# Normalized offset features turned back to channels, GELU with scale and bias there, and the offset product on TensorE

## The chip, the cores and the metric

The kernel runs on one core of a Trainium2 chip, in one launch. The metric is the time of one execution in microseconds (us) of device time; the figure for a kernel is the median of several executions. Engines are named as in the profile: PE is TensorE (matrix products; PEld are its weight loads), DVE is VectorE, ACT is ScalarE, POOL is GpSimd, SP is SyncE, which here only issues DMAs.

## The reference, cut to what matters

Four images of 32 x 32 pixels with 384 channels pass through four layers, each with a group normalization `_gn` before it and a residual sum. Layer 0 is a deformable attention; the part that the change touches makes its offsets:

```python
q = jnp.einsum('bhwc,cd->bhwd', x, w_q) + b_q
o = lax.conv_general_dilated(q, w_off0, (1, 1), 'SAME', ..., feature_group_count=G) + b_off0
mu = o.mean(-1, keepdims=True)
var = ((o - mu) ** 2).mean(-1, keepdims=True)
o = (o - mu) * lax.rsqrt(var + 0.001) * ln_g + ln_b
o = jax.nn.gelu(o, approximate=False)
o = o.reshape(Bq, Hq, Wq, G, GC)...                 # G = 6 groups of GC = 64 channels
offset = jnp.einsum('bhwc,ct->bhwt', o, w_offp)     # w_offp: 64 x 2, the same for each group
offset = jnp.tanh(offset) * jnp.array([Hq / 2.0, Wq / 2.0], x.dtype)
pos = offset + ref
...
xs = _bilinear_sample(xg, pos)                      # keys and values are made from xs
...
bias = _bilinear_sample(rpe_img, disp)              # disp comes from pos too
```

The rest of layer 0 is an attention of six heads over 1024 keys with that bias. Layer 1 is an attention with a convolution branch and a similarity of groups, layer 2 a box filter, layer 3 a dynamic 3 x 3 convolution. Each layer ends in a residual sum.

## The kernel before

Everything is float32. Channels lie on partitions in KC = 3 tiles of 128 (an image is `[128, 3, 1024]`), or pixels lie on partitions in NJ = 8 tiles of 128 (`[128, 8, 384]`).

Two lanes make the instruction stream. `Front` is layer 0 of an image, `Trunk` layers 1 to 3. Image 0's front runs first and alone. Then a loop takes steps of the trunk of image b and adds steps of the front of image b+1 in proportion to planned costs, the numbers behind each `yield`, so that the front of image 1, 2 or 3 shares the engines with the trunk of the image before it. Within this program a scheduler chooses at build time the order in each engine's queue, except where `keep_in_program_order` (`pin`) holds it. That order is fixed in the built program: in the trace, an instruction that waits holds up those behind it on its engine.

The steps of a front, in `inputs0`, with the lines that the prediction names:

- `normed` loads the image's pixels, turns them to channels (copies by ACT, L570), does the group normalization (bn_stats L313; sums over groups on PE, L343, 14 records a time, with 128x128 weights and one column; root on ACT, L366; scaling on DVE, L374), turns the result to pixels (ACT, L594) and writes it to the table `pairs` in DRAM, from which the samples are gathered. For image 0 it also fills the table's borders (ACT's queue, L237) and makes the table of the position bias: DVE works on it in L185 to L192, ACT's queue writes `half` (L193) and then `strips` (L198, six DMAs).
- The queries: a dense product on PE (L393), copied by ACT into `qpad` (L623, three times).
- The offset convolution, three channel tiles of 72 matmuls each (L642), copied by ACT with its bias (L650).
- 24 transposes to pixels (PE, L661), and copies by ACT into `oall` (L665).
- The layer normalization over channels, all on DVE except the root (ACT, L683): per pixel tile one subtraction of the mean and product with ln_g (L692), and one product with 1/std and sum with ln_b (L695). ln_g and ln_b are rows copied to all partitions, since channels lie along the free axis here.
- GELU on ACT per pixel tile (L699).
- `positions`: for each of the two coordinates one product on DVE of the whole tile with w_offp (L478), and a reduction over each group's 64 channels (L479); Tanh on ACT (L480); the positions (L484) and some forty small DVE operations up to the index of the samples `sidx` (L526) and that of the bias `widx`.
- 48 gathers by POOL (L712), eight blocks of six, weighted on DVE (L725) and turned back to channels by PE (L739).

Image 0 does the normalization, GELU and `positions` in two parts of four pixel tiles; images 1 to 3 in one part of eight. The products (L478) write to a work tile `tmp` that has a buffer of the tag `a12`; there are two of these buffers, and large tiles of the front share them in turn. PSUM has two large buffers of `[128, 1024]` (`big`) and four of `[128, 512]` (`bank`), for both lanes.

While the fronts of images 1, 2 and 3 do these steps, the trunk is at the start of layer 1 (`inputs1`): gate (L393, copies L1142), convolution taps on DVE (L1154, L1156), queries and keys by PE (L1168) with copies by ACT or DVE (L1178), norms (L1208 on PE; maximum and reciprocal on DVE, L1220 and L1221), and the first scores (L1322 on PE, maximum on DVE L1330, exponential on ACT L1331).

The functions that the diff touches, and what calls them:

Of the kernel before, what the change touches and what calls it, by code (L numbers as in the profile page):

```python
# [20 lines left out]
AF = mybir.ActivationFunctionType  # L21
ALU = mybir.AluOpType
# [4 lines left out]
P = 128  # L27
# [45 lines left out]
class Net:  # L73
# [33 lines left out]
    def consts(self):  # L107
        nc, a = self.nc, self.a
        self.ident = self.ct([P, P], "ident")
        make_identity(nc, self.ident)  # L110
        self.ones = self.ct([P, P], "ones")
        nc.gpsimd.memset(self.ones, 1.0)
        self.eps = self.ct([P, 2], "eps")
        for i, v in enumerate((1e-5, 1e-3)):
            nc.gpsimd.memset(self.eps[:, i : i + 1], v)

        self.cols = self.ct([P, KC, NCOL], "cols")
        nc.sync.dma_start(self.cols, a["cols"].rearrange("(k p) v -> p k v", p=P))

        self.boff = self.ct([P, KC, 2], "boff")  # L120
        src = a["cols"].rearrange("(k g c) v -> g c k v", g=2, c=GC)
        for g in range(2):
            for h in range(2):
                nc.scalar.dma_start(
                    self.boff[GC * h : GC * (h + 1), :, g], src[g, :, :, C_BOFF]
                )
        self.rows = self.ct([P, NROW], "rows")
        nc.sync.dma_start(self.rows, a["rows"].partition_broadcast(P))
        self.blk = self.ct([P, P], "blk")
        nc.scalar.dma_start(self.blk, a["blk"])  # L130

        self.hsum = self.ct([P, 32], "hsum")
        nc.gpsimd.memset(self.hsum, 0.0)
        nc.vector.tensor_copy(self.hsum[:, 0:4], self.blk[:, 0::32])
        self.hall = self.ct([KC * 32, P], "hall")
        nc.gpsimd.memset(self.hall, 0.0)
        for k in range(KC):
            nc.sync.dma_start(self.hall[32 * k : 32 * k + 4, :], a["blk"][0::32, :])
        self.sel = self.ct([81, 9, 25], "sel")
        nc.scalar.dma_start(self.sel, a["sel"])  # L140
        self.xmask = self.ct([P, 25], "xmask")
        nc.scalar.dma_start(self.xmask, a["xmask"])
        self.wnorm = self.ct([P, HW], "wnorm")
        nc.scalar.dma_start(self.wnorm, a["wnorm"].partition_broadcast(P))
        nc.vector.tensor_scalar(self.wnorm, self.wnorm, 0.2, None, ALU.mult)
        self.ref = self.ct([P, 2, NJ], "ref")
        nc.scalar.dma_start(self.ref, a["ref"])
        self.gofs = self.ct([P, 2, G], "gofs")
        nc.scalar.dma_start(self.gofs, a["gofs"].partition_broadcast(P))
        for g in range(G):  # L150
            nc.gpsimd.memset(self.gofs[:, 1, g : g + 1], float(g * NSTRIP * STRIP))

        self.wa = self.ct([P, KC, 81], "Wa")
        nc.sync.dma_start(self.wa, a["Wa"].rearrange("(k p) d -> p k d", p=P))


        self.gam = self.ct([P, 2], "gam")
        nc.scalar.activation(
            self.gam[:, 0:1], self.rows[:, R_SCAL + 2 : R_SCAL + 3], AF.Sigmoid
        )  # L160
        nc.vector.tensor_scalar(
            self.gam[:, 1:2], self.gam[:, 0:1], -1.0, 1.0, ALU.mult, ALU.add
        )

        self.half = self.ct([P, 2], "half")
        nc.vector.tensor_scalar(
            self.half, self.rows[:, R_SCAL : R_SCAL + 2], 0.5, None, ALU.mult
        )
# [247 lines left out]
class Front(Lane):  # L416
# [48 lines left out]
                nc.sync.dma_start(self.x1[b % 2][rows, :], x)  # L465
                yield 6

    def positions(self, oall, js, tmp, w4, sidx):


        nc, v = self.nc, self.nc.vector
        NC = len(js) * G
        cols = slice(js.start * G, js.stop * G)
        og = oall[:, js.start : js.stop, :].rearrange("p j (g c) -> p (j g) c", g=G)
        th = self.wt([P, 2, NC], "ix_th")
        for t in range(2):
            wrow = self.rows[:, R_WOFFP + t * GC : R_WOFFP + (t + 1) * GC]
            v.tensor_tensor(tmp, og, bc(wrow, 1, NC), ALU.mult)  # L478
            v.tensor_reduce(th[:, t, :], tmp, AX.X, ALU.add)  # L479
        nc.scalar.activation(th, th, AF.Tanh)  # L480
        s = lambda tag, dt=F32: self.wt([P, 2, NC], tag, dt=dt)
        pos = s("ix_pos")
        for t in range(2):
            v.scalar_tensor_tensor(  # L484
                pos[:, t].rearrange("p (j g) -> p j g", g=G),
                th[:, t].rearrange("p (j g) -> p j g", g=G),
                HW / 2.0,
                bc(self.ref[:, t, js.start : js.stop], 2, G),
                ALU.mult,
                ALU.add,  # L490
            )
        qi, gt = s("ix_qi", I32), s("ix_gt")

        def floor(out, q, top):

            v.tensor_copy(qi, q)
            v.tensor_copy(out, qi)
            v.tensor_tensor(gt, out, q, ALU.is_gt)
            v.tensor_tensor(out, out, gt, ALU.subtract)
            v.tensor_scalar(out, out, float(top), 0.0, ALU.min, ALU.max)  # L500


        q, qc, fl, al = s("ix_q"), s("ix_qc"), s("ix_fl"), s("ix_al")
        v.tensor_scalar(q, pos, 0.5, None, ALU.add)
        v.tensor_scalar(qc, q, 0.0, float(HW + 1), ALU.max, ALU.min)
        floor(fl, qc, HW)
        v.tensor_tensor(al, q, fl, ALU.subtract)
        v.tensor_scalar(al, al, 0.0, 1.0, ALU.max, ALU.min)
        one = self.wt([P, 2, NC], "ix_one")
        v.tensor_scalar(one, al, -1.0, 1.0, ALU.mult, ALU.add)  # L510
        edge = self.wt([P, 2, NC], "ix_edge")
        v.tensor_scalar(edge[:, 0, :], fl[:, 0, :], 1.0, None, ALU.is_ge)
        v.tensor_scalar(edge[:, 1, :], fl[:, 0, :], float(HW - 1), None, ALU.is_le)
        wx = self.wt([P, 2, NC], "ix_wx")
        v.tensor_tensor(wx[:, 0, :], one[:, 0, :], edge[:, 0, :], ALU.mult)
        v.tensor_tensor(wx[:, 1, :], al[:, 0, :], edge[:, 1, :], ALU.mult)
        for lr in range(2):
            v.tensor_tensor(w4[:, cols, lr, 0], wx[:, lr, :], one[:, 1, :], ALU.mult)
            v.tensor_tensor(w4[:, cols, lr, 1], wx[:, lr, :], al[:, 1, :], ALU.mult)
        fi = self.wt([P, len(js), G], "ix_fi")  # L520
        fi2 = fi.rearrange("p j g -> p (j g)")

        def index(out, hi, lo, mul, which):
            v.scalar_tensor_tensor(fi2, hi, float(mul), lo, ALU.mult, ALU.add)
            v.tensor_tensor(fi, fi, bc(self.gofs[:, which, :], 1, len(js)), ALU.add)
            v.tensor_copy(out, fi2)  # L526

        index(sidx[:, cols], fl[:, 1, :], fl[:, 0, :], HW, 0)

        u = s("ix_u")
        v.tensor_scalar(u, pos, -1.0, 2.0 * NWIN - 17.0, ALU.mult, ALU.add)
        v.tensor_scalar(u, u, 0.0, 2.0 * NWIN, ALU.max, ALU.min)
        floor(fl, u, 2 * NWIN - 1)
        f = self.f[:, :, :, cols]
        v.tensor_tensor(f[:, 0], u, fl, ALU.subtract)
        v.tensor_scalar(f[:, 1], f[:, 0], -1.0, 1.0, ALU.mult, ALU.add)
        v.tensor_scalar(q, fl, 0.25, None, ALU.mult)
        floor(qc, q, NSTRIP - 1)  # L540
        v.scalar_tensor_tensor(
            fl[:, 0, :], qc[:, 0, :], float(STRIP - 4), fl[:, 0, :], ALU.mult, ALU.add
        )
        index(self.widx[:, 0, cols], fl[:, 1, :], fl[:, 0, :], WROW, 1)

        v.tensor_scalar(fi2, fi2, float(HW // 2 * WROW), None, ALU.add)
        v.tensor_copy(self.widx[:, 1, cols], fi2)
# [60 lines left out]
    def inputs0(self, b):  # L608
# [61 lines left out]

        parts = 2 if b == 0 else 1
        size = NJ // parts
        tmp = self.wt([P, NJ * G, GC], "a12", 2)[:, 0 : size * G]
        w4 = self.wt([P, NJ * G, 2, 2], "w4")
        sidx = self.wt([P, NJ * G], "sidx", 1, I32)
        for part in range(parts):
# [11 lines left out]
            )  # L688
            v.reciprocal(rstd, rstd)
            for i, j in enumerate(js):  # L690
                o = oall[:, j, :]
                v.scalar_tensor_tensor(  # L692
                    o, o, mv[:, j, 0:1], self.rows[:, R_LNG : R_LNG + C], ALU.subtract, ALU.mult
                )
                v.scalar_tensor_tensor(  # L695
                    o, o, rstd[:, i : i + 1], self.rows[:, R_LNB : R_LNB + C], ALU.mult, ALU.add
                )
            for j in js:
                nc.scalar.activation(oall[:, j, :], oall[:, j, :], AF.Gelu)  # L699
            yield 25 / parts  # L700
            self.positions(oall, js, tmp, w4, sidx)
            yield 20 / parts


# [1162 lines left out]
```

## Time and profile before

| | us |
|---|---|
| median of 4 runs | 4708.06 |
| lowest and highest of them | 4704.38, 4716.64 |
| the profiled execution's own time | 4703.28 |
| its span in the profile | 4701.5 |
| PE busy | 4157.6 (88%) |
| DVE busy | 3209.5 (68%) |
| ACT busy | 2295.4 (49%) |
| POOL busy | 944.2 (20%) |

The profiled execution took 1.8 us more than its span, the time that lies outside it. The mean granted clock of PE was 0.927 of the full one. In the rows of the profile a line number such as L479 is a line of the kernel; `out<-in` are the program's tiles, and `xN` says how many instructions the row sums. A timeline's row begins with start and duration in us, and ends, in square brackets, with the time that the engine stood idle before it and what ended that.

### The profile page before, as it was taken

To read this page: it belongs to the slowest core of one execution; us is meant where nothing else is said; L and a number is where in the kernel's file an instruction comes from. 1 tells how busy PE (TensorE), PEld (TensorE's weight loads), DVE (VectorE), ACT (ScalarE), POOL (GpSimd) and SP (SyncE) were. 2 spreads that over 40 slices of the span, in tenths; PEclk is the share of its full clock that TensorE was granted. 3 is DMA by queue.
4 is the path that set the end of the run, shared out by engine and by line. 5 is a ranking of instruction groups with operands and counts; after the bars stand their busy time and mean duration, and the time that the engine had idled before them with its cause. 6 is when DMAs were issued, how large, how long until landed. Compare 5 with 4: busy or idle time off the path is not lost. (4 is left out here: it accounts for less than half of the span.)

```text
span 4701.5 us, 46786 instructions
## 1 busy us (share of the span) xinstructions
PE 4157.6 (88%) x15704; PEld 1781.7 (38%) x15704; DVE 3209.5 (68%) x6013; ACT 2295.4 (49%) x3631; POOL 944.2 (20%) x946
## 2 busy tenths in 40 slices
PE   5477788999999988899999989799999998999998
PEld 2222233333333353333333444343333335343444
DVE  3499755777878727577878753768787784565654
ACT  2166433566665323456666432346565651455532
POOL 1533204211212103311212110422121211000000
PEclk8688988999999988999999989899999998999998
DMA  6435234321212143321212124432121213311011
GB/s 125 131 112 151 69 98 130 90 62 55 70 43 64 63 138 126 109 64 49 82 51 65 49 81 125 147 93 58 29 79 50 75 37 111 110 26 32 19 40 41
DMA packets 231729, 369.98 MB, mean 79 GB/s; under 512 B 117507, under 2 KB 164704, under 8 KB 231488
## 3 DMA queue, kind: packets, MB, share of 16 engines
q1 hardware_dynamic: 170472, 200.51, 14.5%
q0 software_dynamic: 39936, 145.53, 10.4%
q10 hardware_dynamic: 21080, 20.96, 1.8%
q8 instruction: 124, 2.03, 0.2%
q14 instruction: 117, 0.96, 0.1%
HBM read 287.41 MB, written 79.78 MB: 78 GB/s over the span
## 5 line engine op out<-in xcount | busy, mean ns | idle before, releaser
L1479 PE MATMUL bank<-whole,sg 128*128 128x512 f32 (+3 forms) x2304 | 858.4, 507 | 6.3 <-POOL sg L1432 4.4
L1488 DVE SCALAR_TENSOR_TENSOR e<-bank,gam,e 128x512 f32<-128x512 f32 x768 | 561.8, 748 | 439.3 <-ACT gf L1487 157.7
L1331 ACT ACTIVATE big<-big,nmax 128x1024 f32<-128x1024 f32 x384 | 418.7, 1090 | 393.9 <-DVE nmax L1330 346.0
L1457 ACT ACTIVATE e<-big 128x1024 f32<-128x1024 f32 x384 | 379.8, 1019 | 413.4 <-PE big L1449 407.6
L1479 PEld LDWEIGHTS bank<-whole,sg 128*128 128x128 f32 x2304 | 405.3, 198 | 371.1 <-issue 283.1
L1330 DVE TENSOR_REDUCE nmax<-big 128x1 f32<-128x1024 f32 x384 | 454.4, 1218 | 57.6 <-PE big L1322 38.6
L797 POOL DMA_INDIRECT win<-strips,widx x288 | 308.4, 1071 | 684.0 <-DVE z L810 410.9
L1432 POOL TENSOR_SCALAR sg<-whole,gam 128x512 f32<-128x512 f32 x192 | 149.5, 781 | 1451.1 <-PE bank L1479 1014.7
L1449 PE MATMUL big<-qa,ka 64*128 64x512 f32 x1536 | 423.5, 623 | 9.6 <-ACT big L1331 9.3
L1322 PE MATMUL big<-k,q 32*128 32x512 f32 x1536 | 326.1, 680 | 70.5 <-ACT e L1457 40.5
L818 PE MATMUL bank<-qpad,kz 128*128 128x512 f32 x576 | 282.9, 620 | 12.5 <-DVE e L1488 12.5
L712 POOL DMA_INDIRECT gat<-pairs,sidx x192 | 205.4, 1070 | 418.2 <-DVE sidx L526 238.0
L853 PE MATMUL bank<-lg,va 128*64 128x512 f32 x576 | 266.5, 607 | 15.0 <-ACT lg L851 14.9
L853 PE MATMUL bank<-lg,ones 128*64 128x512 f32 x576 | 265.8, 607 | 0.0
L815 DVE SCALAR_TENSOR_TENSOR lg<-z,bias_f,lg 128x512 f32<-128x512 f32 x288 | 220.0, 772 | 39.0 <-ACT lg L814 36.8
L809 ACT ACTIVATE z<-win,bias_f 128x528 f32<-128x528 f32 x288 | 208.2, 738 | 66.4 <-DVE lg L815 30.7
L1449 PEld LDWEIGHTS big<-qa,ka 64*128 64x128 f32 x1536 | 137.9, 186 | 265.9 <-issue 156.2
L810 DVE SCALAR_TENSOR_TENSOR z<-win,bias_f,z 128x528 f32<-128x528 f32 x288 | 214.1, 760 | 26.6 <-ACT z L809 19.4
L850 DVE TENSOR_TENSOR lg<-lg,tb 128x512 f32<-128x512 f32 x288 | 187.1, 695 | 42.4 <-ACT tb L843 42.4
L1421 PE MATMUL bank<-e,vs 128*32 128x512 f32 x1536 | 206.7, 604 | 0.9 <-DVE vs L1415 0.9
L819 DVE TENSOR_TENSOR lg<-bank,lg 128x512 f32<-128x512 f32 x288 | 191.8, 683 | 22.1 <-PE bank L818 21.0
L814 ACT ACTIVATE lg<-z,bias_f 128x512 f32<-128x512 f32 x288 | 200.3, 718 | 12.3 <-PE bank L853 5.6
(302 smaller groups left out, 6634.3 us busy)
## 6 DMA issues: line engine op xcount, KB each, us to landing
pairs<-xn SPq DMA_DIRECT2D x64, 192.0 KB
q<-qd SPq DMA_DIRECT2D x48, 256.0 KB
w<-in_gmat SPq DMA_DIRECT2D x16, 576.0 KB
w<-in_w_off SPq DMA_DIRECT2D x12, 576.0 KB
w<-in_Wqkv SPq DMA_DIRECT2D x12, 576.0 KB
a<-in_x SPq DMA_DIRECT2D x16, 384.0 KB
x<-a ACTq DMA_DIRECT2D x4, 1536.0 KB
win<-strips,widx POOLq DMA_INDIRECT x384
```

Of the source, the lines that this page charges most:

```text
L797: nc.gpsimd.indirect_dma_start(out=win, out_offset=None, in_=self.strips[:, :], in_offset=bass.IndirectOffsetOnAxis(ap=self.widx[:, q, c : ...
L810: v.scalar_tensor_tensor(z, wv[:, 1 : HH + 1, 0 : HW + 1], sc(0, 1), z, ALU.mult, ALU.add)
L815: v.scalar_tensor_tensor(lg, z[:, :, 1 : HW + 1], sc(0, 0), lg, ALU.mult, ALU.add)
L818: nc.tensor.matmul(ps, kz[:, j * P : (j + 1) * P], both, start=True, stop=True)
L853: nc.tensor.matmul(po[out, :], w, lf, start=j == 0, stop=j == NJ - 1)
L1322: nc.tensor.matmul(ps[r][:, h * 512 : (h + 1) * 512], self.q4[rows, i * P : (i + 1) * P], self.k4[rows, 0:512], start=True, stop=True,)
L1330: v.tensor_reduce(nmax[:, r, i : i + 1], ps[r], AX.X, ALU.max, negate=True)
L1331: nc.scalar.activation(ps[r], ps[r], AF.Exp, bias=nmax[:, r, i : i + 1], accum_out=den[:, r, i : i + 1],)
L1449: nc.tensor.matmul(ps[:, r, :], ka[rows, j * P : (j + 1) * P], qa[rows, cols], start=True, stop=True,)
L1457: nc.scalar.activation(e, ps, AF.Exp)
L1479: nc.tensor.matmul(ps[:, (mid - i0) * P :], sg[:, r, m, :], sim[:, h, r, m, (mid - i0) * P :], start=m == 0, stop=m == 1,)
L1488: v.scalar_tensor_tensor(e[:, r, :], ps, self.gam[:, 1:2], e[:, r, :], ALU.add, ALU.mult, accum_out=tot[:, r, h : h + 1],)
```

## The change

After the change the layer normalization in pixels does only its subtraction and product, `(o - mean) * rstd`, as one DVE instruction per pixel tile. 24 transposes on PE, in groups that fill a `big` each, turn the result to channels. There ln_g and ln_b are one number per partition, so that ACT's GELU applies them as scale and bias while it reads PSUM; it writes a tile `ge` that takes the place of `tmp` among the `a12` buffers. The offsets are matmuls: for each pixel tile and channel tile, 128 pixels of `ge` are the weights and a constant `offp` of `[128, 4]` is the moving operand. It holds w_offp for the upper and the lower 64 channels in columns of their own, so that the four results are two coordinates for two groups. The 24 matmuls (12 for each part of image 0) fill one `bank`, and Tanh reads it. `tmp` and DVE's products and reductions are gone. The constants `ln` and `offp` are loaded at the start, by six DMAs on ACT's queue, after a memset by POOL.

```diff
@@ consts
         nc.sync.dma_start(self.rows, a["rows"].partition_broadcast(P))
+        self.ln = self.ct([P, 2, KC], "ln")
+        for i, at in enumerate((R_LNG, R_LNB)):
+            nc.scalar.dma_start(
+                self.ln[:, i, :], a["rows"][at : at + C].rearrange("(k p) -> p k", p=P)
+            )
+        self.offp = self.ct([P, 4], "offp")
+        nc.gpsimd.memset(self.offp, 0.0)
+        for h in range(2):
+            for t in range(2):
+                at = R_WOFFP + t * GC
+                nc.scalar.dma_start(
+                    self.offp[GC * h : GC * (h + 1), 2 * h + t : 2 * h + t + 1],
+                    a["rows"][at : at + GC].rearrange("(c o) -> c o", o=1),
+                )
@@ positions
-    def positions(self, oall, js, tmp, w4, sidx):
+    def positions(self, ge, js, w4, sidx):
...
-        og = oall[:, js.start : js.stop, :].rearrange("p j (g c) -> p (j g) c", g=G)
+        ps = self.bank()
+        for i in range(len(js)):
+            for k in range(KC):
+                at = (i * KC + k) * 4
+                nc.tensor.matmul(
+                    ps[:, at : at + 4],
+                    ge[:, k, i * P : (i + 1) * P],
+                    self.offp,
+                    start=True,
+                    stop=True,
+                )
         th = self.wt([P, 2, NC], "ix_th")
-        for t in range(2):
-            wrow = self.rows[:, R_WOFFP + t * GC : R_WOFFP + (t + 1) * GC]
-            v.tensor_tensor(tmp, og, bc(wrow, 1, NC), ALU.mult)
-            v.tensor_reduce(th[:, t, :], tmp, AX.X, ALU.add)
-        nc.scalar.activation(th, th, AF.Tanh)
+        nc.scalar.activation(
+            th, ps[:, 0 : 2 * NC].rearrange("p (n t) -> p t n", t=2), AF.Tanh
+        )
@@ inputs0
-        tmp = self.wt([P, NJ * G, GC], "a12", 2)[:, 0 : size * G]
+        gelus = self.wt([P, KC, N], "a12", 2)
...
             for i, j in enumerate(js):
-                o = oall[:, j, :]
-                v.scalar_tensor_tensor(
-                    o, o, mv[:, j, 0:1], self.rows[:, R_LNG : R_LNG + C], ALU.subtract, ALU.mult
-                )
-                v.scalar_tensor_tensor(
-                    o, o, rstd[:, i : i + 1], self.rows[:, R_LNB : R_LNB + C], ALU.mult, ALU.add
-                )
-            for j in js:
-                nc.scalar.activation(oall[:, j, :], oall[:, j, :], AF.Gelu)
+                v.tensor_scalar(
+                    oall[:, j, :], oall[:, j, :],
+                    mv[:, j, 0:1], rstd[:, i : i + 1],
+                    ALU.subtract, ALU.mult,
+                )
+            ge = gelus[:, :, js.start * P : js.stop * P]
+            for k in range(KC):
+                ps = self.big()[:, 0 : size * P]
+                for i, j in enumerate(js):
+                    nc.tensor.transpose(
+                        ps[:, i * P : (i + 1) * P], oall[:, j, k * P : (k + 1) * P], self.ident
+                    )
+                nc.scalar.activation(
+                    ge[:, k, :],
+                    ps,
+                    AF.Gelu,
+                    bias=self.ln[:, 1, k : k + 1],
+                    scale=self.ln[:, 0, k : k + 1],
+                )
             yield 25 / parts
-            self.positions(oall, js, tmp, w4, sidx)
+            self.positions(ge, js, w4, sidx)
```

More of the change, by code (lines that the diff above doesn't have):

```diff
@@ L690, in inputs0 @@
             for i, j in enumerate(js):
-                o = oall[:, j, :]
-                v.scalar_tensor_tensor(
-                    o, o, mv[:, j, 0:1], self.rows[:, R_LNG : R_LNG + C], ALU.subtract, ALU.mult
-                )
-                v.scalar_tensor_tensor(
-                    o, o, rstd[:, i : i + 1], self.rows[:, R_LNB : R_LNB + C], ALU.mult, ALU.add
-                )
-            for j in js:
-                nc.scalar.activation(oall[:, j, :], oall[:, j, :], AF.Gelu)
+                v.tensor_scalar(
+                    oall[:, j, :],
+                    oall[:, j, :],
+                    mv[:, j, 0:1],
+                    rstd[:, i : i + 1],
+                    ALU.subtract,
+                    ALU.mult,
+                )
+            ge = gelus[:, :, js.start * P : js.stop * P]
[11 more added lines that the diff above has]
+                    scale=self.ln[:, 0, k : k + 1],
+                )
             yield 25 / parts
-            self.positions(oall, js, tmp, w4, sidx)
+            self.positions(ge, js, w4, sidx)
             yield 20 / parts
```

## The prediction

> **What bounds the kernel now.** I read the engines' busy shares first, then a table of windows round the code that the change touches, then the timelines of those windows. PE is busy 88% of the 4701.5 us span, so over the whole program only time in which PE stands idle, or works for nothing, can be won. But the change touches four stages only, and each has its own limit. The table of windows shows them (columns: window, length, busy us and instruction count of PE, weight loads, DVE, ACT and POOL, then granted clock, DMA share, GB/s):
>
> ```profile
> 0.00:80.00 80.00, 56.77 (x328) 29.57 (x328) 12.14 (x29) 15.70 (x27) 6.56 (x21) 0.89 0.88 170
> 80.00:111.00 31.00, 3.94 (x28) 2.58 (x24) 28.11 (x69) 13.06 (x24) 0.23 (x1) 0.65 0.07 20
> ...
> 660.00:680.00 20.00, 20.00 (x51) 7.54 (x50) 20.00 (x34) 10.86 (x17) 0.00 (x0) 1.00 0.53 149
> 680.00:700.00 20.00, 13.75 (x39) 4.95 (x37) 20.00 (x24) 7.13 (x10) 0.00 (x0) 0.92 0.25 82
> ```
>
> Image 0's front runs alone: from 80 to 111 us DVE is busy 28.11 of 31, PE only 3.94, and the gathers wait for it. Image 1's front shares its time with the trunk: from 660 to 680 PE and DVE are both full, then DVE stays full while PE has gaps. Images 2 and 3 repeat this at about 1800 and 2930 us.
>
> Image 0's chain, from the timeline: last convolution pass, both tanh, the index of part 0, first gather.
>
> ```profile
> 55.28 25.12 PE L642 MATMUL big<-qpad,w 64*64 64x512 f32 x216 [0.52 <-issue]
> ...
> 100.61 0.24 ACT L480 ACTIVATE ix_th<-ix_th 128x48 f32<-128x48 f32 x1 [1.14 <-DVE ix_th L479]
> ...
> 110.31 0.17 DVE L526 CAST sidx<-ix_fi 128x24 int32<-128x24 f32 x1
> ...
> 110.77 1.16 POOL L712 DMA_INDIRECT gat<-pairs,sidx  x1 [91.78 <-DVE ix_fl L497]
> ...
> 112.32 0.24 ACT L480 ACTIVATE ix_th<-ix_th 128x48 f32<-128x48 f32 x1 [8.46 <-DVE ix_th L479]
> ```
>
> The index of part 0 comes 9.7 us after its tanh, because DVE does part 1's work in between. From 110.77 to about 180 us 48 gathers follow one another at some 1.25 us. After them the heads keep DVE busy for 271.35 of the 280 us from 260 to 540. So an earlier first gather moves all that follows, one for one.
>
> The joint stage of image 1, DVE's timeline:
>
> ```profile
> 682.88 3.35 DVE L479 TENSOR_REDUCE ix_th<-a 128x48 f32<-128x3072 f32 x1
> ...
> 687.26 3.34 DVE L1221 RECIPROCAL inv<-inv 96x512 f32<-96x512 f32 x1
> 690.52 0.26 DVE L484 SCALAR_TENSOR_TENSOR ix_pos<-ix_th,ref 128x48 f32<-128x48 f32 x2
> 690.70 1.22 DVE L1330 TENSOR_REDUCE nmax<-big 128x1 f32<-128x1024 f32 x1
> ...
> 693.02 4.95 DVE L1221 RECIPROCAL inv<-inv 96x768 f32<-96x768 f32 x1
> ...
> 701.82 0.19 DVE L526 CAST sidx<-ix_fi 128x48 int32<-128x48 f32 x1
> ```
>
> The tanh runs at 686.25, but its reader L484 stands behind a reciprocal of the trunk until 690.52. So up to 4.27 us of a later tanh are free; what comes later still holds L484, and with it L1330, the second L1221 and the index, all queued behind it on DVE.
>
> **DVE's part of the change.** Per image 8 normalizations of 0.593 us (L692) and 8 of 0.609 us (L695) go: 9.6 us. Eight scalings of 128x384 come instead; L374's 0.81 us for 128x1024 gives an estimate of 0.31 us each, 2.5 us. Two products of 3.35 us (L478) and two reductions of 3.34 us (L479) go too, 13.4 us. DVE is relieved of 9.6 + 13.4 - 2.5 = 20.5 us per image.
>
> **PE's part.** 24 transposes come, like L661's, which issue six in 0.82 us: 0.137 us each, 3.3 us. And 24 matmuls with 128x128 weights and 4 columns in 4-byte numbers. No such shape runs now; the nearest is L343 with one column, 14 records, of which a matmul makes two:
>
> ```profile
> 1556.78 1.72 PE L343 MATMUL bank<-gn_d,w 128*128 128x1 f32 x14
> ...
> 26.58 3.12 PE L343 MATMUL bank<-gn_d,w 128*128 128x1 f32 x14 [0.93 <-DVE gn_d L362]
> ```
>
> That is 0.123 us a record at its fastest and 0.223 us in a cold stretch. 48 records: 5.9 or 10.7 us. PE gains 9.2 us warm, 14.0 cold. In the joint stage I take warm (clock 1.00 from 660 to 680, 0.92 after), in image 0 cold (0.65 from 80 to 111).
>
> [...]
>
> **ACT's part.** Eight GELU of 0.51 us from SBUF (4.1 us) become three of 128x1024 from PSUM; L1331's 1.09 us gives 3.3 us. In image 0 they are six of 128x512, like L650's 0.687 us: 4.1 us. Tanh reads PSUM, 0.28 us as now. So ACT is even. Each GELU now waits for a PSUM buffer that PE must fill, and on ACT the next copies queue behind it; the joint stage has ACT at about half, so I give this nothing, up to 1 us if it is seen.
>
> **Constants.** Six loads of 4-byte elements go on ACT's queue, plus one small memset on POOL. They cost issue time on ACT in the first 15 us, where ACT waits for x anyway (3.11 us before 14.90); uncovered it would be some 0.3 us each (L193's issue), 2 us.
>
> **What moves in image 0's opening.** The rebuilt instruction orders, set side by side, are alike on every engine outside the four stages and the opening. In the opening the work on the rpe table (DVE's L185 to L192, ACT's issue of half) goes behind the group normalization. Now ACT holds its last five copies of x behind it: they wait 2.83 us for DVE's L185 and end at 20.2. Ahead of it they would end at about 18, after x's last landing. Then the six strip loads, which block ACT's queue for 12.64 us now (39.59 to 53.25), stand after the second L623 instead of the first. So the convolution can start at about 48 instead of 55.28, but its second third waits for the third L623, blocked until about 59. I get an end of the convolution near 75.6 instead of 80.33: 4.7 us won. Bounds: nothing, if the third L623 comes late by as much as the first came early, and 7 us, the whole advance of the start.
>
> **Image 0 between convolution and gathers.** From the first transpose back (80.33), the tanh of part 0 comes now at +20.3, that of part 1 at +32.0, the index of part 0 at +30.0. After the change DVE's chain is short: square root at +6.5, the GELU after a 1.28 us table load at +8.8, then two more table loads for part 1's square root and GELU, third GELU of part 0 at +13.7. Twelve matmuls at 0.446 us each are 5.3 us, cold: tanh of part 0 at about +18.2, of part 1 at +26.5. But DVE's new order has part 1's first use of its tanh (the line that is L484 now) ahead of part 0's index. So the index of part 0 waits for part 1's tanh and comes about nine small operations later, 0.9 us: +27.5 against +30.0. Gain 2.5 us, not the 10 that DVE's relief suggests; bounds -1 (matmuls behind late buffers) and +5. Image 0 together: 4.7 + 2.5, about 7 us won, from 11 won to 1 lost.
>
> **Images 1 to 3.** In the new order PE has the 24 transposes among the trunk's L1168 and the 24 matmuls in one run after them. Adding the 9.2 us to PE's full stretch, and counting what stands before it, I put the matmuls at 684.4 to 690.0 and the tanh at 690.1 to 690.4. DVE, relieved, reaches the first L1221 by 682.9 and ends it at 686.7, then waits 3.8 us for the tanh. L484 then runs at 690.5, as now; L1330 about 0.9 later, as its scores come later from PE, the second L1221 1.0 later, index at 702.8 instead of 701.82. DVE's 20.5 us are thus spent waiting. PE's delay ends in its two gaps there (5.95 us before L1168, waiting for DVE's L1178; 4.73 before the first L739). Cost: 1 us per image; bounds 5 lost (matmuls cold) and 3 won (index ahead of the second reciprocal). Three images: 3 us lost, from 15 lost to 9 won.
>
> **Sum.** -7 + 3 = -4 us. Profiled: own time 4703.28 becomes 4699.3. The runs' median is 4708.06, 4.8 us above the profiled one, so I forecast 4704. Ends: -11 - 9 = -20 and +1 + 15 = +16, so 4688 to 4724. About 0.2%, 9.4 us, is what a measurement can tell from no change here.
>
> **Rivals.** (1) PE bound, slower. PE is full from 641 to 692; if its two gaps stay as long as they are, since the DVE work that ends them moves with it, the 9.2 us come through in full, three times 27.6 us, less 7 of image 0: 4729. Against it: the gaps end with DVE's L1178 and with the gathers, and DVE has been relieved. It decides from where the matmuls end later than 690.5, where L484 stands now: from there on each us moves the index one for one. Chance 0.27, part of it at half that size, 4718.
> (2) DVE's relief counts, faster. DVE is full from 660 to 700; if the matmuls came early in PE's queue, the tanh could come by 680 and the index some 10 us earlier, three times, and with image 0's 7 us that is 4671. For it speaks only DVE's full row; against it the order of PE's queue, which puts the matmuls after the trunk's L1168. Chance 0.13.
> (3) Image 0 alone counts, the stages of images 1 to 3 even: 11 us won, 4697. Chance 0.2; it shades into my case, which has 0.4.
>
> **The numbers.** Faster by over 0.2% takes all of (2), most of (3): 0.32. Slower takes (1) and the cold end: 0.28. Within: 0.40. The range stretches beyond my own ends to take the half-sized (1) and a third of (2): 4684 to 4726.
>
> **What would show it.** After: first gather near 103.5 us; in image 1 DVE idle about 3.8 us before the first L484, tanh near 690, index near 703; small matmuls at 0.12 us a record there and 0.22 in image 0. I am wrong if the index of image 1 moves by more than 5 us either way, if the first gather is not earlier, or if a stage outside these four moves the end.

## The result: slower by 0.28%

| | us | runs |
|---|---|---|
| median before | 4708.94 | 78 |
| median after | 4721.60 | 52 |
| ratio of the times, 95% interval | 1.0028 (1.0021 to 1.0035) | |
| profiled execution after: own time, span | 4713.76, 4711.9 | |

The change costs 13 us (10 to 16). Single executions of either kernel spread over some 35 us, so the experiments below are compared by many executions each, and by their profiles stage by stage.

The profile after, in the table of windows that was shown of before (same columns):

```profile
80.00:111.00 31.00, 21.28 (x112) 17.96 (x104) 12.67 (x58) 13.93 (x23) 0.46 (x1) 0.64 0.07 20
...
660.00:680.00 20.00, 19.47 (x68) 8.04 (x67) 9.32 (x23) 9.14 (x10) 0.00 (x0) 1.00 0.55 168
680.00:700.00 20.00, 20.00 (x75) 11.63 (x76) 9.89 (x14) 7.60 (x10) 0.00 (x0) 0.74 0.09 33
```

DVE is relieved as promised: 9.32 and 9.89 us busy where it had been full. PE is now full from 680 to 700 us, and its granted clock there is 0.74 instead of 0.92. The loss begins with this drop.

Image 0's chain after (PE, ACT, DVE and POOL in the timelines; L667, L648, L503, L551 and L751 are before's L642, L623, L480, L526 and L712):

```profile
49.66 7.96 PE L667 MATMUL big<-qpad,w 64*64 64x512 f32 x72
63.14 18.31 PE L667 MATMUL big<-qpad,w 64*64 64x512 f32 x144 [5.52 <-ACT qpad L648]
...
101.83 0.21 ACT L503 ACTIVATE ix_th<-bank 128x48 f32<-128x48 f32 x1 [3.37 <-PE bank L495]
...
108.99 0.21 ACT L503 ACTIVATE ix_th<-bank 128x48 f32<-128x48 f32 x1 [4.57 <-PE bank L495]
...
110.08 0.17 DVE L551 CAST sidx<-ix_fi 128x24 int32<-128x24 f32 x1
...
110.54 1.16 POOL L751 DMA_INDIRECT gat<-pairs,sidx  x1 [93.85 <-DVE ix_pos L509]
```

The convolution starts 5.6 us sooner, but waits 5.52 us for its second input and ends at 81.4 us, 1.1 later than before. The index of part 0 does wait for part 1's tanh: on DVE, part 1's first use of it (L509, 109.23 us) stands ahead of it. The first gather comes at 110.54 instead of 110.77.

The joint stage of image 1 after, on DVE (L1260 is the reciprocal, L509 the first use of the tanh, L1369 the maximum, L551 the index):

```profile
681.51 3.35 DVE L1260 RECIPROCAL inv<-inv 96x512 f32<-96x512 f32 x1
689.59 0.33 DVE L509 SCALAR_TENSOR_TENSOR ix_pos<-ix_th,ref 128x48 f32<-128x48 f32 x2 [4.73 <-ACT ix_th L503]
694.34 1.22 DVE L1369 TENSOR_REDUCE nmax<-big 128x1 f32<-128x1024 f32 x1 [4.43 <-PE big L1361]
...
696.67 4.95 DVE L1260 RECIPROCAL inv<-inv 96x768 f32<-96x768 f32 x1
...
705.47 0.18 DVE L551 CAST sidx<-ix_fi 128x48 int32<-128x48 f32 x1
```

DVE waits 4.73 us for the tanh, which is no loss (L509 stands at 689.59, before's L484 at 690.52). But then it waits another 4.43 us for the scores, and everything behind it is late: the index by 3.65 us. PE's timeline of the same time shows why:

```profile
682.50 6.77 PE L495 MATMUL bank<-offp,a 128*128 128x4 f32 x48
689.20 2.07 PE L1361 MATMUL big<-k,q 32*128 32x512 f32 x2
691.20 1.06 PE L1247 MATMUL bank<-sq,hsum 128*32 128x256 f32 x2
692.19 2.08 PE L1361 MATMUL big<-k,q 32*128 32x512 f32 x6
694.20 6.56 PE L1207 MATMUL bank<-whole,w 128*128 128x512 f32 x12
```

The small matmuls (L495) are followed by the scores (L1361) at half speed. Windows of the same profile, cut where the clock changes (PE's busy time first, granted clock the third number from the end), for images 1, 2 and 3:

```profile
682.50:686.30 3.80, 3.80 (x36) 3.80 (x35) 2.36 (x1) 1.88 (x2) 0.00 (x0) 1.00 0.49 172
686.30:696.50 10.20, 10.20 (x28) 5.24 (x28) 2.49 (x9) 4.10 (x5) 0.00 (x0) 0.50 0.00 0
1820.10:1822.90 2.80, 2.80 (x28) 2.80 (x26) 2.32 (x1) 1.88 (x2) 0.00 (x0) 1.00 0.44 165
1822.90:1836.60 13.70, 13.70 (x39) 7.73 (x39) 4.18 (x11) 4.40 (x6) 0.00 (x0) 0.50 0.05 15
2956.60:2959.60 3.00, 3.00 (x29) 2.96 (x27) 2.40 (x1) 1.88 (x2) 0.00 (x0) 0.99 0.46 165
2959.60:2973.20 13.60, 13.60 (x38) 7.54 (x38) 4.26 (x11) 4.40 (x6) 0.00 (x0) 0.50 0.03 12
```

In all three stages the clock falls to half 2.8 to 3.8 us after the first small matmul, and stays there for 10.2 to 13.7 us, while PE is busy without a gap. In the profile of before the clock was full up to 696.7 us. Then it fell there too, for 13.7 us:

```profile
696.80:710.30 13.50, 9.13 (x14) 2.68 (x14) 12.44 (x42) 5.79 (x10) 6.20 (x7) 0.50 0.38 127
```

The same falls stand in before at 1829.9 and 2959.7 us, again for 13.7 us each. All three begin inside the 5.95 us in which PE waits for DVE's L1178, and PE was busy for only two thirds of them. Over each stage as a whole (640 to 850, 1780 to 1990 and 2905 to 3120 us) the mean granted clock is 0.89, 0.90 and 0.90 before and 0.89, 0.89 and 0.88 after. So the change adds little time at half clock. It brings the fall forward, into a stretch in which PE is full and DVE waits for PE's scores.

Where the time went, from the starts of like instructions in the two profiles (after less before, medians): 3.1 us ahead at 540 us, 0.8 ahead at 650; then 4.3 us lost in the stage of image 1 (up to 800 us), 7.3 in that of image 2 (1780 to 1930), 6.9 in that of image 3 (2900 to 3100). Some 5 us come back between 3580 and 3800 us; all other profiles of this study gain 2 to 8 us on before there as well, so that is most likely a loss of before's one profiled execution and no gain of the change.

### The profile page after: what moved, and what is told of

The parts are those of the page before. It is cut to its first block, busy times and chain, and to the rows that moved or that the text cites. A ratio compares the mean times of both kernels' runs of the same rounds, so it can differ in the third digit from the quotient of the medians.

```text
span 4711.9 us, 47291 instructions
## 1 busy us (share of the span) xinstructions
PE 4197.9 (89%) x15992; PEld 1822.6 (39%) x15992; DVE 3141.1 (67%) x5961; ACT 2294.8 (49%) x3614; POOL 947.4 (20%) x947
## 5 line engine op out<-in xcount | busy, mean ns | idle before, releaser
L1370 ACT ACTIVATE big<-big,nmax 128x1024 f32<-128x1024 f32 x384 | 418.5, 1090 | 416.8 <-DVE nmax L1369 365.3
L1369 DVE TENSOR_REDUCE nmax<-big 128x1 f32<-128x1024 f32 x384 | 454.1, 1217 | 81.1 <-PE big L1361 53.7
L1361 PE MATMUL big<-k,q 32*128 32x512 f32 x1536 | 327.9, 679 | 65.1 <-ACT e L1496 39.0
L751 POOL DMA_INDIRECT gat<-pairs,sidx x192 | 207.9, 1083 | 440.8 <-DVE sidx L551 255.1
L858 DVE TENSOR_TENSOR lg<-bank,lg 128x512 f32<-128x512 f32 x288 | 191.9, 683 | 24.5 <-PE bank L857 23.5
```

The lines of the kernel that those rows point to most:

```text
L1361: nc.tensor.matmul(ps[r][:, h * 512 : (h + 1) * 512], self.q4[rows, i * P : (i + 1) * P], self.k4[rows, 0:512], start=True, stop=True,)
L1369: v.tensor_reduce(nmax[:, r, i : i + 1], ps[r], AX.X, ALU.max, negate=True)
L1370: nc.scalar.activation(ps[r], ps[r], AF.Exp, bias=nmax[:, r, i : i + 1], accum_out=den[:, r, i : i + 1],)
```

## The experiments

My theory after the result: PE's clock falls because of the narrow matmuls, and what costs time is everything that runs at half clock behind them. Rivals: PE simply has more work in a stage where it is full (work), and the new opening of image 0 costs too (opening). "Before" in each row below was run on the same chip with the experiment.

| run | ratio to before, 95% interval | median us (before) |
|---|---|---|
| front0_only | 0.9985 (0.9973 to 0.9997) | 4696.01 (4703.63) |
| joint_only | 1.0012 (0.9996 to 1.0029) | 4712.38 (4703.63) |
| wide128 | 0.9953 (0.9937 to 0.9969) | 4679.62 (4703.63) |
| early | 1.0034 (1.0020 to 1.0047) | 4718.23 (4703.63) |
| wide32 | 1.0020 (1.0002 to 1.0038) | 4712.74 (4705.94) |
| wide64 | 0.9949 (0.9932 to 0.9966) | 4684.16 (4705.94) |
| front_fixed | 1.0015 (0.9999 to 1.0032) | 4712.97 (4705.94) |
| front_fixed_wide128 | 0.9960 (0.9947 to 0.9974) | 4687.77 (4705.94) |
| few | 0.9973 (0.9957 to 0.9989) | 4692.62 (4706.42) |
| early128 | 1.0019 (1.0004 to 1.0034) | 4713.29 (4706.42) |
| wide64_free | 0.9959 (0.9943 to 0.9974) | 4684.73 (4706.42) |
| front0_fixed | 0.9989 (0.9974 to 1.0005) | 4699.16 (4706.42) |

**The change in halves.** `inputs0` takes the new path for some images only:

```diff
+        new = b == 0        # front0_only;  joint_only: b > 0
```

> Image 0 as in the changed kernel with its constants, images 1 to 3 as before. The theory (clock): the whole loss lies in the stages of images 1 to 3, where the small matmuls bring PE's clock to half; without them there the time is that of before less what image 0 won (3.5 us in the two profiles, 0.9 us after the next clock window), so 4705 to 4708. A rival (opening): the constants and the new opening cost too, because the convolution ends 1.1 us later; then the time is above 4711.

> Image 0 as before (but with the constants loaded), images 1 to 3 as in the changed kernel. The theory (clock): 4.4, 7.0 and 6.5 us lost in the three stages, as in the profile of the changed kernel, 18 us in all, so 4723 to 4728; the granted clock falls to half about 3 us after the first small matmul in each of the three stages. The rival (opening): less than 10 us lost, under 4718.

Image 0 alone is 0.15% faster (0.03 to 0.27), so neither the constants nor the new opening cost anything in the end; its profile stands 2.2 us ahead at 640 us (the changed kernel's 0.8). So the loss is not image 0's. That images 1 to 3 lose by themselves joint_only does not show: its ratio, 1.0012, is within its interval of nothing, its median is 9 us above before, where 15 to 20 were expected, and by the bounds set beforehand (under 4718) it falls to the rival. Nor do the halves add up: 0.15% won and 0.12% lost are not 0.28% lost. Its executions lie in two heaps, 4684 to 4699 us at a mean clock of 0.931 to 0.934, and 4712 to 4718 us at 0.926 to 0.932. Its profile (4696.79 us) belongs to the lower heap, although it has the half clock behind the small matmuls in all three stages (0.66 from 680 to 700 us): the stages cost 3.7, -1.0 and 2.3 us there. So the fall behind the matmuls does not fix the time of an execution alone. What else makes the heaps I did not find out.

**The width alone.** The matmuls keep their number, their weights and their place; zeros widen the moving operand. Since a scheduler that sees other shapes makes other queues, the queues of the changed kernel were written into the kernel as ordering edges (without waits), and each engine's order is the same to the instruction.

```diff
-        self.offp = self.ct([P, 4], "offp")
+        self.offp = self.ct([P, 128], "offp")
...
-                    ps[:, at : at + 4],
+                    ps[:, at : at + wide],      # 128 for images 1 to 3, 4 for image 0
                     ge[:, k, i * P : (i + 1) * P],
-                    self.offp,
+                    self.offp[:, 0:wide],
```

Each matmul writes its four sums and zeros behind them, which the next one overwrites.

> The changed kernel with every queue in its order, but in images 1 to 3 the moving operand of the 24 matmuls is padded with zeros from 4 to 128 columns (the result is the same). The theory (clock): matmuls that stream 128 columns keep the clock at full speed; the 48 records take 5.9 us, not 6.8 to 7.6, the scores behind them run at full speed, DVE's wait for the scores shrinks from 4.4 us to about 1, the index of image 1 comes at about 702.5, not 705.5, and the time falls by 3 to 5 us for each image, to 4707 to 4712. The rival (work): what counts is only PE's additional time; the wider matmuls take as long or longer, the time stays at 4721 or rises.

wide128's windows, and its PE and DVE timelines (L496 the offset matmuls, L1362 the scores, L1370 the maximum, L552 the index):

```profile
680.00:700.00 20.00, 20.00 (x88) 10.94 (x86) 14.40 (x28) 7.95 (x12) 0.00 (x0) 1.00 0.09 33
700.00:720.00 20.00, 16.46 (x44) 6.32 (x43) 15.02 (x36) 6.95 (x13) 14.91 (x14) 0.86 0.67 223
720.00:740.00 20.00, 19.88 (x68) 9.23 (x66) 19.05 (x22) 7.97 (x15) 16.04 (x14) 0.89 0.65 216
740.00:760.00 20.00, 16.18 (x51) 7.45 (x49) 13.46 (x20) 9.64 (x20) 15.73 (x15) 0.91 0.67 190
```

```profile
681.28 5.52 PE L496 MATMUL bank<-offp,a 128*128 128x128 f32 x48
686.73 1.12 PE L1362 MATMUL big<-k,q 32*128 32x512 f32 x2
687.78 0.62 PE L1248 MATMUL bank<-sq,hsum 128*32 128x256 f32 x2
688.33 1.13 PE L1362 MATMUL big<-k,q 32*128 32x512 f32 x6
```

```profile
689.53 1.23 DVE L1370 TENSOR_REDUCE nmax<-big 128x1 f32<-128x1024 f32 x1 [2.09 <-PE big L1362]
...
700.66 0.18 DVE L552 CAST sidx<-ix_fi 128x48 int32<-128x48 f32 x1
```

With 32 times the columns the 48 records take 5.52 us, less than the narrow ones' 6.77. The clock is full from 680 to 700 us; the scores take 2.7 us, not 5.1; the index comes 4.8 us earlier than in the changed kernel. The whole kernel is 0.47% faster than before. Work as the whole cause is refuted: there is no less of it for PE here, and it wins 35 us on the changed kernel (by the two ratios, 0.9953 against 1.0028). The queues are the same, so the columns alone make this difference. That is over twice what I expected. The gain goes on behind the index. Before, for the same windows:

```profile
700.00:720.00 20.00, 14.46 (x32) 4.35 (x32) 15.95 (x44) 6.67 (x13) 13.76 (x14) 0.74 0.55 186
720.00:740.00 20.00, 16.92 (x46) 7.35 (x46) 9.11 (x11) 5.62 (x10) 15.43 (x16) 0.74 0.51 159
740.00:760.00 20.00, 15.15 (x37) 6.02 (x37) 15.02 (x16) 7.19 (x14) 11.37 (x11) 0.70 0.47 161
```

While the gathers run, PE's clock is 0.86 to 0.91 in wide128 and 0.70 to 0.74 in before, and the 48 gathers of image 1 start within 67.3 us (701.12 to 768.44) instead of 75.7 (702.28 to 777.99); in the changed kernel they take 75.8. The first weighting comes 10.0 us behind the first gather, not 12.9 (after: 11.9). So DVE's relief seems to pay fully only with the higher clock; why the clock falls less often in this stretch, the runs do not show.

**How wide.** The same with 32 and with 64 columns.

> As wide128 (every queue in the changed kernel's order), but the moving operand of images 1 to 3 is padded to 32 columns. [...] A rival (any width above a few columns is enough): the clock stays at full speed and the time is that of wide128, about 20 us below before.

> As wide32 with 64 columns: half the streaming of wide128. [...]

By the clock theory I expected of 32 columns what 4 do, a fall to half about 3 us after the first matmul and a time 8 to 14 us above before; for 64 I left open whether they would do this or what 128 do (about 20 us below before, clock 1.00 from 680 to 700 us). 64 columns do what 128 do. With 32 the clock does fall in all three stages, but later (684.4, 1821.1 and 2947.5 us, 5.8 to 6.3 us after the first matmul instead of 2.8 to 3.8) and for 6.8 or 6.9 us only. Its windows of 20 us from 680, 1815 and 2941 us:

```profile
680.00:700.00 20.00, 20.00 (x72) 9.71 (x72) 12.59 (x34) 6.91 (x10) 0.00 (x0) 0.83 0.09 33
1815.00:1835.00 20.00, 20.00 (x81) 10.57 (x80) 12.95 (x26) 7.48 (x10) 0.00 (x0) 0.83 0.10 34
2941.00:2961.00 20.00, 20.00 (x80) 10.51 (x79) 13.02 (x24) 7.49 (x10) 0.00 (x0) 0.83 0.09 33
```

Its executions lie between 4686 and 4735 us. In these profiles, one execution for each width, the half clock behind the matmuls thus follows the columns: 4, 32, 64 and 128 give 10 to 14, 7, 0 and 0 us. The index follows too. This is how much later than in before the first gather of each image comes, each counted from the start of its own stage (by the like instructions around 650, 1770 and 2895 us):

| columns (run) | image 1 | image 2 | image 3 |
|---|---|---|---|
| 4 (after) | 4.4 us | 5.2 us | 5.2 us |
| 32 (wide32) | 2.6 us | 2.3 us | 2.2 us |
| 64 (wide64) | 0.8 us | 0.7 us | 0.8 us |
| 128 (wide128) | 0.8 us | 0.7 us | 1.8 us |

At full clock the delay is close to the 1 us an image that I had forecast. The time of a whole execution is looser: wide32's profiled one took 4686.27 us, the lowest of its twelve (median 4712.74), at a mean clock of 0.933, where the two slowest had 0.925.

The falls of the changed kernel come 2.8 to 3.8 us after the first small matmul, joint_only's after 2.5, 4.2 and 5.2 us. PE was not idle before them: in the changed kernel it was busy for 3.80 us of 3.80, 2.80 of 2.80 and 3.00 of 3.00 between the first small matmul and the fall. In before the falls begin while PE stands idle, inside the 5.95 us of waiting for L1178. So half clock followed idle time in before and a row of matmuls with few columns in the changed kernel; what the two have in common, the runs do not show.

**How many.**

```diff
+                nc.tensor.matmul(       # images 1 to 3: 8 matmuls, not 24
+                    ps[:, i * 12 : (i + 1) * 12], ge[:, i % KC, i * P : (i + 1) * P], self.ident[:, 0:12],
+                    start=True, stop=True)
```

> The changed kernel, but images 1 to 3 do only 8 of the 24 offset matmuls, of 12 columns (for each pixel tile one of its three channel tiles, against the first 12 columns of the unit matrix), so that two thirds of the sums are left out; the queues' order is the changed kernel's but for one place. The theory (clock): 16 records last 2 us, less than one of the 3.4 us steps in which the clock is seen to change, so mostly the clock does not fall behind them; then the time is that of wide128 less the 3.5 to 4 us of PE work left out, 18 to 30 us below before. The rival (work): PE is relieved of 16 of 24 matmuls, 5 us an image at what they took, 12 to 15 us in all, so 0 to 4 us below before.

13 us below before, between the two expectations. The clock stayed full in image 1 (1.00 from 680 to 700 us), but fell in image 2 for 3.4 us and in image 3 for 6.8 (from 1807.8 and 2937.6 us; mean clock 0.88 from 1806 to 1820 us, 0.76 from 2936 to 2950). So a fall followed even 1.9 us of narrow matmuls, in two of three stages; the theory's number assumed that mostly it would not. The profile is of the fastest of the twelve executions, 4676.71 us.

**The place.** `early` puts GELU and offsets out in one step, so that the scheduler places the matmuls, the tanh and the index right behind the GELU; `early128` adds the 128 columns.

```diff
-            yield 25 / parts
             self.positions(ge, js, w4, sidx)
-            yield 20 / parts
+            yield 45 / parts
```

> The changed kernel, but the offset matmuls of each image are put out in the same step as the GELU, so that the scheduler places them, the tanh and the index right behind the GELU in all queues, ahead of the trunk's last gate product and reciprocals. The theory (clock) with a chance for the relief of DVE: the index of image 1 comes some 20 us earlier (about 680, not 705.5), while the trunk's queries and keys come about 10 us later at half clock; since the gathers follow the index, the time falls by up to 10 us an image, 4690 to 4712. The rival (work): the trunk's layer 1 sets the pace there, and 7 us an image are lost as before or more, 4720 to 4735.

> The kernel early with 128 columns in images 1 to 3 (here the scheduler's own order). early was 14 to 16 us slower than before, with the clock at half twice inside its PE run. If that was the clock: 15 to 25 us less than early, at or below before. If it was the place (the trunk's queries and keys 20 us later, the first weighting 50 us behind the first gather): no more than 8 us less, still above before.

The index of image 1 came at 678.28 us, 23.5 sooner than before, and won nothing: the first weighting on DVE started at 729.35 us instead of 715.21, since the trunk's work, now 20 us later, stands ahead of it in DVE's queue, and the gathers stop for it after 18. So this lies with the rival, not with the theory. With 128 columns early gains 0.15%, within the intervals: what costs here is mostly the place. The clock is not out of it, though. In early's profile it fell twice in the stage of image 1: from 657.7 us, while PE stood idle for 6.64 us waiting for DVE's scalings (mean clock 0.57 from 657 to 665 us), and from 671.4 us, behind the small matmuls (0.57 from 671 to 679). In early128 the second fall is gone and the first is still there (656.7 to 663.5 us).

**Is it the held order?**

> wide64 without the queue orders held: the scheduler sees 64 columns and puts the second reciprocal of the trunk ahead of the first use of the tanh on DVE, and splits the scores on PE. The theory (clock): the clock stays at full speed here too; the index comes 3 to 6 us later than in wide64 since 4.95 us of reciprocal stand ahead of it, and the time is 8 to 20 us below before. The rival (order): the held order is what won, not the clock; then it is within 5 us of before or above it.

No: 0.9959, the same as wide64 within the intervals, and here too the clock is 1.00 from 680 to 700 us. The index did not come later, either (700.80 us in wide64). On DVE the second reciprocal now runs while the tanh is awaited, and the first use of the tanh (L510) follows it at once:

```profile
685.87 4.95 DVE L1261 RECIPROCAL inv<-inv 96x768 f32<-96x768 f32 x1
690.74 0.25 DVE L510 SCALAR_TENSOR_TENSOR ix_pos<-ix_th,ref 128x48 f32<-128x48 f32 x2
...
700.19 0.19 DVE L552 CAST sidx<-ix_fi 128x48 int32<-128x48 f32 x1
```

So the plain edit, without ordering edges, is the version to use: 64 columns in images 1 to 3.

**Image 0.** The loads of the constants move to SP's queue behind image 0's queries, and an ordering edge puts part 0's index ahead of part 1's first use of its tanh.

```diff
+            if js.start:
+                self.tc.add_manual_dep(ins.ins, self.ixdone, ...)   # behind part 0's index, order only
...
-        index(sidx[:, cols], fl[:, 1, :], fl[:, 0, :], HW, 0)
+        self.ixdone = index(sidx[:, cols], fl[:, 1, :], fl[:, 0, :], HW, 0).ins.name
```

> The changed kernel with narrow matmuls, but the loads of the constants go on SP's queue after image 0's queries (so that the opening has the order of before), and part 0's index stands ahead of part 1's first use of its tanh on DVE. The theory for image 0: the convolution ends at about 80.4 us as before, tanh of part 0 at about 100.6, its index 3 us later at about 104, first gather at about 104.3 instead of 110.5, so 6 us less than the changed kernel: 3 to 9 us above before. A rival (the gathers of part 0 only wait longer for part 1's index, or the heads wait for the bias table): less than 2 us won, 10 to 14 above before.

> front_fixed and wide128 together, in the same queue orders. If image 0 and the stages of images 1 to 3 add up: 6 us below wide128, 26 to 30 us below before, a ratio of 0.994. If part of image 0's gain is lost to the clock or to the trunk's pace: as wide128, 0.995 to 0.996.

> Image 0 as in front_fixed, images 1 to 3 as before. If image 0's gain is carried through the program: 8 us below before (as its profile had at 640 us), ratio 0.998. If it is lost behind image 0 (front_fixed_wide128 was not faster than wide128): within 4 us of before.

The mechanism is as expected: in front_fixed the first gather comes 5.4 us sooner than in the changed kernel,

```profile
104.67 0.17 DVE L546 CAST sidx<-ix_fi 128x24 int32<-128x24 f32 x1
```

```profile
105.13 1.16 POOL L761 DMA_INDIRECT gat<-pairs,sidx  x1 [86.17 <-DVE ix_fl L517]
```

and all three profiles stand 8 to 9 us ahead of before at 500 us. Its worth at the end is not settled. front_fixed is 6 us better than the changed kernel against before, front0_fixed 5 us better than before, each within its interval of nothing; front_fixed_wide128 is not faster than wide128. In front_fixed's profile 7 us are lost in the stage of image 1, and more in those of images 2 and 3. Whether the advance is given back in the joint stages or only drowns in the spread of the clock, these runs do not tell.

## Why the prediction was wrong

The forecast was a gain of 4 us; 13 were lost. The time lies in the range only because the range reached to the rivals: 4721.6 is close to the half-sized price of the first, 4718.

- **The step that failed: "In the joint stage I take warm".** The small matmuls were priced at 0.123 us a record from L343's row at 1556.78. That row lasts 1.72 us at a clock of 1.00; in the three runs of 48 records the clock fell to 0.50 after 3.8, 2.8 and 3.0 us. They took 6.77, 7.62 and 7.56 us instead of 5.9. The worse half is what I priced at nothing: all that stands behind them on PE at half clock. The first scores took 5.1 us instead of 2.7, so L1330 came at 694.34 and not 0.9 us late at 691.6, and the index 3.65 us late and not 1.0. Three stages cost 4.3, 7.3 and 6.9 us instead of 1 each; their sum, 18, is beyond the bound of 15 that I gave for cold matmuls. With 64 columns, where the clock stays full, the index comes 0.7 to 0.8 us late: the rest of the chain was right.
- **What held in that stage.** The place of the matmuls (684.4 to 690.0 forecast, 682.5 to 689.2 measured), the tanh (690.1 to 690.4; 689.3), DVE's idle wait (3.8; 4.73), and L484's place (690.5; 689.59). The queue orders were read rightly; the speed was not.
- **The transposes.** They were not what struck: 24 of them ran among the trunk's matmuls from 661.8 to 669.1 us at a clock of 1.00, and wide128 has the same transposes and no fall behind them. What struck were the narrow matmuls.
- **Image 0's opening.** The convolution was to end 4.7 us sooner; it ended 1.1 later. The third copy of the queries came at 61.95 us, not at 59, because four of the strip DMAs held ACT's queue for 15.2 us; the bound "nothing" was on the wrong side of zero.
- **Image 0's index.** Forecast at 27.5 us behind the convolution, measured at 28.7 (before 30.0). The tanh of part 1 was at 27.6 (forecast 26.5), and the index waited for it, as read from the order. Together image 0 won 0.2 us at the first gather and 3.1 at 540 us, instead of 7. (The two upper ends for image 0, 7 and 5 won, add up to 12, not 11.)
- **DVE's new scalings** took 0.475 us, not 0.31; it waits there anyway.
- **The rivals.** The first named the right sign, and PE, but its price was PE's 9.2 us of work; wide128 has this work and is faster than before. The second, that DVE's relief counts, was right that something is there to win, but wide128 wins 22 us and not 37, and not by the index, which comes 1.2 us sooner than in before and not 10; the narrow matmuls let nothing of it through.

## What to carry to other kernels

A matmul with a handful of columns can cost more than its own time: here the clock fell to half after 2.8 to 3.8 us of them in a row, and the bill was paid by the matmuls behind, whose first scores took 5.1 us instead of 2.7. Where more columns do not lengthen the records, widen the moving operand with zeros; here 48 records took 5.44, 5.47 and 5.52 us with 32, 64 and 128 columns, and 64 or 128 turned 0.28% lost into 0.4 to 0.5% won. A price taken from a short row need not hold for a long run: ask what the clock will do over the length of the new run, and who runs next.

## What I had not expected of the hardware

- PE's clock fell while PE was busy without a gap, where the columns were few: 0.50 from 2.8 to 3.8 us on with 4 columns, half clock from 5.8 to 6.3 us on with 32, none behind the matmuls with 64 and 128, at an equal number of records of like length (6.77 us for 48 with 4 columns, 5.52 with 128).
- The stage of image 1 went with the clock well behind the place of the matmuls too: with 0.86 to 0.91 instead of 0.70 to 0.74 while its gathers ran, they started within 67.3 us instead of 75.7 (wide128 and before). This part varies: in image 2 of wide64_free, whose clock was full at the small matmuls, the gathers took 83.7 us.
